# A graph layer on one core: 68 instead of 72 column copies on VectorE, a second bank for the turned comparison, and a later addition of the sums

## The chip, the core and the metric

The kernel runs on one core of a Trainium2 chip. The metric is the device time of one execution in microseconds (us); the median of the runs is given. The engines are TensorE (PE), VectorE (DVE), ScalarE (ACT), GpSimd (POOL) and SyncE (SP). Each takes its instructions in order from a queue of its own; what orders them among each other are semaphores.

## What is computed

12500 nodes have 64 features each (x), and 400000 edges, sorted by their destination, have 16 attributes each.

```python
m_in = concat([x[src], x[dst], edge_attr], axis=-1)     # 64 + 64 + 16
h = silu(m_in @ W1 + b1)
messages = silu(h @ W2 + b2)
agg = segment_sum(messages, dst, num_segments=12500)
z = silu(concat([x, agg], axis=-1) @ W3 + b3)
out = layernorm(x + z, axis=-1)
```

## The kernel before

The edges are cut into 3125 tiles of 128, and eight tiles make an **oct**: 391 turns of the main loop, whose order on PE, ACT, VectorE and SP is written out by hand (`tc.manual_schedule`). Two tiles make a **pair**, and pairs are laid side by side over the 128 partitions.

Since the edges are sorted, the eight tiles of an oct point at a short window of 48 nodes. `compare_nodes` (L433, VectorE) compares each edge's destination with the 48 and gives a 0/1 matrix `eh`; `turn` (L451, PE) turns it into a PSUM bank (`ph`, pool `psh`), and `turned` (L461, VectorE) copies that to SBUF. `window_product` (L410, PE) multiplies the window's slice of x with its part of W1 into a bank of the pool `mis`, and `window_copy` (L415, VectorE) takes it out. `first_layer` (L486, L489, L490 on PE; L493, the silu to `h`, on ACT) adds the three parts of the first layer; `second_layer` (L502, L504 on PE; L508, the silu to `m`, on ACT) follows two octs later. `add_up` (L517, PE) sums the messages of an oct into one of four slots of a PSUM bank (`sums`, pool `psa`), four octs later; `add_window` (L522, VectorE) adds such a slot to the window's place in `agg`, LAST octs later, with an address from a register.

The sources' features come in three ways, and this is what the engines are mostly busy with:

- POOL gathers 128 rows of x (from oct 12 on, of the product x·W1, made once by `table`, L186 on PE and L189 on ACT, and written to DRAM) with one indirect DMA (L386), one for each tile.
- For some first pairs of an oct, ACT and VectorE copy the columns from x in SBUF one by one, four bytes on 64 partitions: `nc.scalar.copy` (L312) and a `tensor_reduce` over one element (L310). Each address is loaded into a register first (L302): 16 registers at once on ACT, up to 32 on VectorE. `address` (L371, VectorE) makes addresses of 256 indices, one pair. Each pair done in this way saves POOL two gathers.
- For one second pair in sixteen octs, SP fetches the rows singly, 16 in each oct.

How many columns an oct copies is set by two tuples, and the place of VectorE's parts in the loop by their order:

```python
ACOLS = (40, 32)
VCOLS = (32, 0, 32, 8)
RATE = sum(ACOLS) + sum(VCOLS)          # columns per oct, 256 to a pair
...
columns(o, ENG.DVE, 0)                  # behind add_window, compare_nodes
first_layer(o)
window_copy(o + 1)
columns(o, ENG.DVE, 1)
turned(o + 1)
columns(o, ENG.DVE, 2)
columns(o, ENG.DVE, 3)
```

So VectorE's order in oct o is: `bases` (registers for the windows' places, every fourth oct, L395), `add_window`, `compare_nodes` of oct o + 2, 32 columns, `window_copy` of oct o + 1, `turned` of oct o + 1, 32 and 8 columns, then node work and `address`. PE's order is: `turn` and `window_product` of oct o + 1, `first_layer` of o, `add_up` of o - 4, `second_layer` of o - 2, then node work (L548, L553, L558), which is spread over the octs for groups of 512 nodes whose sums are complete.

The eight PSUM banks are: `mis` 2 (window products; in the first twelve octs also `table`'s products and the gathered features that are turned, `pt`), `wrow` 1, `ps1` 2, `ps2` 1, `psh` 1, `psa` 1.

The functions that the diff touches:

Of the kernel before, what the change touches and what calls it, by code (L numbers as in the profile page):

```python
# [9 lines left out]
F32 = mybir.dt.float32  # L10
# [6 lines left out]
PSUM = bass.MemoryType.PSUM  # L17
# [3 lines left out]
P = 128  # L21
G = 4
CT = 24
OT = 8
# [3 lines left out]
AHEAD = 3  # L28
SECOND = 2
THIRD = 4  # L30
LAST = 6
RAW = 12
BEGIN = 6
TABLES = 7
ACOLS = (40, 32)
VCOLS = (32, 0, 32, 8)
ROWS = 16
LOADS = (16, 32)
XADDR = 37344
# [64 lines left out]
def windows(ctx, tc, ident, identb, badi, pa, x, xt, xt2, src_c, src_row, dst_c, dst_row, attr_t, attr_2, base, w1, b1, w2, b2, w3, b3, out, edges):  # L104
# [5 lines left out]
    NO = base.shape[1]  # L110
# [63 lines left out]
    zero = const.tile([P, 1], F32, name="zero")  # L174
    nc.vector.memset(zero, 0.0)

    mis = ctx.enter_context(tc.tile_pool(name="mis", bufs=2, space=PSUM))


    def table(c):  # L180
# [79 lines left out]
    with tc.tile_pool(name="gat", bufs=AHEAD + 2) as gat, \  # L260
# [3 lines left out]
            tc.tile_pool(name="msg", bufs=THIRD - SECOND + 1) as msg, \  # L264
            tc.tile_pool(name="ps1", bufs=2, space=PSUM) as ps1, \
            tc.tile_pool(name="ps2", bufs=1, space=PSUM) as ps2, \
            tc.tile_pool(name="psh", bufs=1, space=PSUM) as psh, \
            tc.tile_pool(name="psa", bufs=1, space=PSUM) as psa, \
            tc.tile_pool(name="cx", bufs=5) as cx, tc.tile_pool(name="cxi", bufs=3) as cxi, \
            tc.tile_pool(name="rx", bufs=2) as rx, tc.tile_pool(name="rxi", bufs=2) as rxi, \  # L270
# [193 lines left out]
        def first_layer(o):  # L464
            c, t0, n, first, last = octs[o]
            n2 = n + n % 2
            k = n2 // 2
            ga = got.pop(o)
            oh, eh = hots.pop(o)
            p1 = ps1.tile([P, OT // 2, P], F32, name="p1")  # L470
            if o < RAW:
                c = 1 if o in pairs else 0
                nc.tensor.matmul(p1[:, :k], xw[o % 3], oh, start=True, stop=False, skip_group_check=True)
                if c:
                    nc.tensor.matmul(p1[:, 0, :], w1d, cols.pop(o), start=False, stop=False, skip_group_check=True)
                pt = mis.tile([P, OT // 2, P], F32, name="mm")
                for i in range(c, k):
                    nc.tensor.transpose(pt[:, i, :], ga[:, 2 * i:2 * i + 2, :].rearrange("p s d -> p (s d)"), ident)
                xg = msg.tile([P, OT // 2, P], F32, name="m")
                nc.vector.tensor_copy(xg[:, c:k], pt[:, c:k])  # L480
                nc.tensor.matmul(p1[:, c:k], w1d, xg[:, c:k], start=False, stop=True, skip_group_check=True)
            else:
                c = 1 if o in pairs else 0
                for i in range(c, k):
                    g2 = single.pop(o) if o in rpairs and i == 1 else ga[:, 2 * i:2 * i + 2, :]
                    nc.tensor.matmul(p1[:, i, :], g2.rearrange("p s d -> p (s d)"), ident,  # L486
                                     is_transpose=True, start=(i == c), stop=False, skip_group_check=True)
                if c:
                    nc.tensor.matmul(p1[:, 0, :], w1d, cols.pop(o), start=False, stop=False, skip_group_check=True)  # L489
                nc.tensor.matmul(p1[:, :k], xw[o % 3], oh, start=False, stop=True, skip_group_check=True)  # L490
            columns(o, ENG.Activation, 0)
            h = work.tile([P, OT // 2, P], F32, name="h")
            nc.scalar.activation(h[:, :k], p1[:, :k], AF.Silu)  # L493
            made[o] = h, eh
# [25 lines left out]
        def add_window(o):  # L520
            a = agg[:, ds(winreg.pop((ENG.DVE, o)), S)]
            nc.vector.tensor_tensor(a, a, sums[:, o % 4, :], op=OP.add)  # L522
# [85 lines left out]
        for q in range(rest):  # L608
            o = lead[due[q]] + LAST - 1
# [40 lines left out]
        def times(lags):  # L650

            at = {}
            for o in range(NO):
                at.setdefault(o + lags.get(NO - 1 - o, lags[None]), []).append(o)
            return at

        seconds = times({None: SECOND, 0: 1, 1: 1, 2: 1})
        adds = times({None: THIRD, 0: 2, 1: 2, 2: 2, 3: 3, 4: 3, 5: 3})
        folds = times({None: LAST, 0: 3, 1: 4, 2: 4, 3: 5})

        for o in range(min(AHEAD, NO)):
            gather(o)
# [14 lines left out]
        with tc.manual_schedule(engines={ENG.PE, ENG.Activation, ENG.DVE, ENG.SP}):  # L677
# [4 lines left out]
            for o in range(NO + 2):  # L682
                if o == 0:
                    sources(0, slice(CT, SCT))
                    nc.sync.dma_start(dc[:, CT:SCT], dst_c[:, CT:SCT])
                for k in parts[3 * o - 3:3 * o] if o else []:
                    n = min(XC, NP - k)
                    nc.scalar.activation(agg[:, k:k + n], zero.to_broadcast([P, n]), AF.Copy)
                if o < 2:
                    for c in parts[2:5] if o == 0 else parts[5:]:  # L690
                        resident(c)
                if o == 3:
                    for s in range(2):
                        nc.scalar.dma_start(w3s[s * D:(s + 1) * D, :], w3[D:2 * D, :])
                    nc.scalar.dma_start(w3x, w3[0:D, :])
                    nc.vector.tensor_copy(b3r, b2p[:, 1:2, :].to_broadcast([3, G, D]))
                if o == 8:
                    nc.scalar.dma_start(dc[:, SCT:], dst_c[:, SCT:])
                if o == RAW:
                    nc.vector.memset(mv, 1.0)  # L700
                    nc.vector.memset(eps, 1e-5)
                index(o + 3)
                rload(o + 3)
                if o % (SCT // OT) == 6 and (o // (SCT // OT) + 1) * SCT < TILES:
                    sources(o // (SCT // OT) + 1)
                if o + AHEAD < NO:
                    gather(o + AHEAD)
                if o + 3 < NO and octs[o + 3][3]:
                    load(octs[o + 3][0])
                if o + 3 < NO:  # L710
                    window_load(o + 3)
                if o + 1 < NO:
                    turn(o + 1)
                if o + 1 < NO - 1:
                    window_product(o + 1)
                if o % 4 == 0 and 4 <= o < NO + 4:
                    bases(ENG.DVE, o - 4)
                for q in folds.get(o, []):
                    add_window(q)
                if o == 1:  # L720
                    relative(CT, SCT)
                if o + 2 < NO:
                    compare_nodes(o + 2)
                columns(o, ENG.DVE, 0)
                if o < NO:
                    first_layer(o)
                for f, a in todo.get(o, []) if o < NO else []:
                    if f is node_silu:
                        f(*a)
                if o == 0:  # L730
                    nc.vector.tensor_copy(b2r, b2p[:, 0:1, :].to_broadcast([3, OT, D]))
                if o + 1 < NO:
                    if o + 1 < NO - 1:
                        window_copy(o + 1)
                    if o + 1 == NO - 2:
                        window_product(o + 2)
                        window_copy(o + 2)
                    columns(o, ENG.DVE, 1)
                    turned(o + 1)
                    columns(o, ENG.DVE, 2)  # L740
                columns(o, ENG.DVE, 3)
                if 10 <= o < 9 + len(cuts):
                    relative(cuts[o - 10], cuts[o - 9])
                if 30 <= o < 30 + 2 * LP and o % 2 == 0:
                    k = (o - 30) // 2
                    part = rel[:, k * TILES // LP:(k + 1) * TILES // LP]
                    nc.vector.tensor_reduce(lims[:, 0, k:k + 1], part, AX.X, OP.min)
                    nc.vector.tensor_reduce(lims[:, 1, k:k + 1], part, AX.X, OP.max)
                if o >= 1:
                    for c in tables[(o - 1) * per:o * per]:  # L750
                        table(c)
                for q in adds.get(o, []):
                    add_up(q)
                for q in seconds.get(o, []):
                    second_layer(q)
                for f, a in todo.get(o, []) if o < NO else []:
                    if f in (node_begin, node_x, node_sums):
                        f(*a)
                address(o + 2)
                raddress(o + 2)  # L760
                rows(o)
                if o < NO:
                    for f, a in todo.get(o, []):
                        if f not in (node_silu, node_begin, node_x, node_sums):
                            f(*a)
                if o == NO - 4:
                    for q in range(rest, NG):
                        node_load(q)
                if o in (NO - 3, NO - 2):
                    for q in (rest,) if o == NO - 3 else range(rest + 1, NG):  # L770
                        node_begin(q, acc if q == rest else mis.tile([P, G, D], F32, name="mm"))
                        for i in range(G):
                            node_x(q, i)
# [279 lines left out]
```

## Time and profile before

| | |
|---|---|
| median of 3 runs | 3539.86 us (3532.58 to 3542.2) |
| the profiled execution | 3546.66 us, of which the span in the profile is 3544.8 us |
| busy share PE / DVE / ACT / POOL | 73% / 72% / 89% / 71% |
| granted clock of PE, mean | 0.671 |
| octs | 391 |

In the profile's rows a group has its line, engine, operation, its tiles (out<-in), shapes and count, then the busy time in us and the mean duration of one in ns, and behind the second bar the engine's idle time ahead of these instructions and what ended it. "issue" is idle time that no wait in the profile accounts for. Rows of the order of time begin with the start and the duration in us; in brackets stands the idle time ahead of them. Rows of the stretches give the stretch, its length, then busy time and number of instructions for PE, weight loads, DVE, ACT and POOL, PE's granted clock, and the DMA share and rate. Rows of a line's instructions give the count, the shortest, median and longest duration in ns, and the first and last start in us. An engine's name with a q (DVEq) stands for its queue: register loads, register arithmetic and waits, which count as no busy time. Register loads are named by L302 (column addresses) and L395 (windows' places).

### The profile page before, as it was taken

The page shows a single profiled execution, that of the slowest core. Times are in us where ns is not written, and L with a number is a line of the kernel's source. Part 1 is how long each engine was busy: PE and PEld are TensorE (multiplying, and loading weights), DVE is VectorE, ACT ScalarE, POOL GpSimd, SP SyncE. Part 2 cuts the span into 40 slices and gives each one's busy share as a digit, 9 for nine tenths or more (in the row PEclk, how much of TensorE's full clock was granted, in tenths as well). Part 3 has the DMA queues.
Part 4 walks back from the last instruction along what each step waited for, and adds up shares of the span by engine and source line. Part 5 has one row for each costly group of instructions (what it writes and reads, how often), then busy time and mean ns, then how long its engine had stood idle before and what let it go on. Part 6 is the DMA issues. An engine that isn't in the chain of part 4 may idle for free. (4 is left out here: it accounts for less than half of the span.)

```text
span 3544.8 us, 111270 instructions
## 1 busy us (share of the span) xinstructions
PE 2574.5 (73%) x15317; PEld 1760.8 (50%) x15317; DVE 2549.4 (72%) x29217; ACT 3167.6 (89%) x27861; POOL 2512.8 (71%) x2666
## 2 busy tenths in 40 slices
PE   7777777877777677777766777777777767766676
PEld 5454454545444455454544544544545444544454
DVE  2777777777777777777777777777777777777772
ACT  2899999999999999999999999999999999999992
POOL 7777776777767767767677677776776777767774
PEclk7766766566667666666676666666666666677666
DMA  5222211212211212111211211112211111112121
GB/s 110 58 41 40 41 39 38 40 36 41 40 41 41 41 37 41 38 37 38 45 42 37 41 38 38 39 39 42 43 39 37 39 40 38 38 40 44 38 41 30
DMA packets 159534, 147.84 MB, mean 42 GB/s; under 512 B 103191, under 2 KB 111532, under 8 KB 158268
## 3 DMA queue, kind: packets, MB, share of 16 engines
q0 software_dynamic: 85024, 87.23, 14.0%
q1 hardware_dynamic: 59670, 45.36, 5.0%
q10 hardware_dynamic: 14086, 8.03, 1.0%
q14 instruction: 627, 5.14, 0.5%
q8 instruction: 127, 2.08, 0.2%
HBM read 133.98 MB, written 6.40 MB: 40 GB/s over the span
## 5 line engine op out<-in xcount | busy, mean ns | idle before, releaser
L386 POOL DMA_INDIRECT ga<-pa,sc x2563 | 2421.8, 945 | 959.5 <-issue 681.6
L312 ACT COPY cx<-xs 64x4 uint8 x27016 | 2709.9, 189 | 150.7 <-issue 122.3
L310 DVE TENSOR_REDUCE cx<-xs 64x4 uint8 x27000 | 1821.9, 140 | 830.9 <-issue 789.7
L451 PE MATMUL ph<-identb,eh 128*96 128x128 bf16 x1563 | 229.0, 291 | 627.0 <-DVE oh L461 618.4
L517 PEld LDWEIGHTS pg<-eh,m 128*64 128x64 f32 x6250 | 289.1, 179 | 769.8 <-DVE agg L522 714.2
L490 PE MATMUL p<-oh,xw 128*128 128x512 f32 (+1 forms) x758 | 651.8, 960 | 0.0
L504 PE MATMUL p<-w2d,h 128*128 128x128 f32 x3126 | 626.8, 362 | 0.0
L504 PEld LDWEIGHTS p<-w2d,h 128*128 128x128 f32 x3126 | 531.3, 257 | 128.4 <-issue 128.4
L517 PE MATMUL pg<-eh,m 128*64 128x48 f32 x6250 | 343.9, 266 | 237.1 <-DVE agg L522 230.1
L451 PEld LDWEIGHTS <-eh 128*96 128x96 bf16 x1563 | 158.4, 169 | 700.2 <-DVE oh L461 689.2
L493 ACT ACTIVATE h<-p 128x512 f32<-128x512 f32 x391 | 232.2, 594 | 110.0 <-PE p L490 88.6
L486 PE MATMUL p<-ident,ga 128*128 128x128 f32 x1282 | 319.9, 384 | 5.2 <-DMA ga<-pa,sc 5.2
L508 ACT ACTIVATE m<-p 128x512 f32<-128x512 f32 x391 | 231.6, 592 | 49.6 <-PE p L504 44.1
L461 DVE COPY oh<-ph 96x512 f32<-96x512 f32 x391 | 263.7, 674 | 5.2 <-PE ph L451 5.2
L486 PEld LDWEIGHTS p<-ident,ga 128*128 128x128 f32 x1282 | 245.1, 206 | 5.9 <-issue 5.8
L410 PE MATMUL mm<-w1bb,xr 65*96 65x128 f32 x782 | 237.3, 401 | 9.1 <-DMA xr<-in_xt 5.6
L433 DVE TENSOR_TENSOR eh<-wrow,dc 128x384 f32<-128x384 f32 x392 | 213.4, 545 | 4.8 <-PE pg L517 4.6
L502 PE MATMUL p<-b2r,one 3*128 3x512 bf16 x391 | 189.6, 485 | 1.7 <-ACT m L508 1.6
L490 PEld LDWEIGHTS p<-oh,xw 128*128 128x128 f32 x758 | 188.3, 304 | 0.0
L410 PEld LDWEIGHTS mm<-w1bb,xr 65*96 65x96 f32 x782 | 150.4, 246 | 10.8 <-DMA xr<-in_xt 6.0
L415 DVE TENSOR_TENSOR xw<-mm,mask 96x128 f32<-96x128 f32 x391 | 109.5, 280 | 22.7 <-PE mm L410 19.6
L489 PE MATMUL p<-cx,w1d 128*128 128x128 f32 x420 | 121.5, 388 | 0.0
(96 smaller groups left out, 921.7 us busy)
## 6 DMA issues: line engine op xcount, KB each, us to landing
rx<-pa SPq DMA_DIRECT2D x5888, 0.2 KB
ga<-pa,sc POOLq DMA_INDIRECT x2563
oh<-in_attr SPq DMA_DIRECT2D x130, 192.0 KB
xr<-in_xt SPq DMA_DIRECT2D x391, 24.0 KB
cxi<-in_src_row SPq DMA_DIRECT2D x211, 1.0 KB
xs<-in_xt ACTq DMA_DIRECT2D x6, 512.0 KB
pa<-v ACTq DMA_DIRECT2D x12, 256.0 KB
xa<-in_x SPq DMA_DIRECT2D x24, 128.0 KB
```

Of the source, the lines that this page charges most:

```text
L310: nc.vector.tensor_reduce(to, frm[:, :, None], AX.X, OP.max)
L312: nc.scalar.copy(to, frm)
L386: nc.gpsimd.indirect_dma_start(out=ga[:, i, :], out_offset=None, in_=x if o < RAW else pa[:, :], in_offset=bass.IndirectOffsetOnAxis(ap=sc ...
L410: nc.tensor.matmul(pw[:E, :], winrow[o], w1bb.rearrange("k s m -> k (s m)"), start=True, stop=True)
L451: nc.tensor.matmul(ph[:E, i, :], eh[:, i, :, 1], identb, start=(i == 0), stop=(i == k - 1), skip_group_check=True)
L461: nc.vector.tensor_copy(oh[:E, :], ph[:E, :(n + 1) // 2].rearrange("p i e -> p (i e)"))
L486: nc.tensor.matmul(p1[:, i, :], g2.rearrange("p s d -> p (s d)"), ident, is_transpose=True, start=(i == c), stop=False, skip_group_check=True)
L490: nc.tensor.matmul(p1[:, :k], xw[o % 3], oh, start=False, stop=True, skip_group_check=True)
L493: nc.scalar.activation(h[:, :k], p1[:, :k], AF.Silu)
L504: nc.tensor.matmul(p2[:, 2 * i:2 * i + 2, :].rearrange("p s d -> p (s d)"), h[:, i, :], w2d, start=False, stop=(i == k - 1), skip_group_ch ...
L508: nc.scalar.activation(m[:, :n2], p2[:, :n2], AF.Silu)
L517: nc.tensor.matmul(pg[s * D:(s + 1) * D, :], m[:, i, :], eh[:, i // 2, :, s], start=(i < 2), stop=(i >= n - 2), skip_group_check=True)
```

## The change

VectorE copies 68 columns in each oct where it copied 72: the last part of VCOLS has 4 columns for 8. With that RATE is 140, so a pair's 256 columns take 1.83 octs. `psh` has two banks and `mis` one; in the first twelve octs the gathered features are turned in a bank of `psh`. `add_window` moves in VectorE's order from ahead of `compare_nodes` to behind `turned`, and LAST, the number of octs after which it is due, falls from 6 to 5 (with its exceptions at the end, `folds`); the node work that needs the sums is placed by LAST and comes an oct earlier.

```diff
-LAST = 6
+LAST = 5
...
-VCOLS = (32, 0, 32, 8)
+VCOLS = (32, 0, 32, 4)
...
-    mis = ctx.enter_context(tc.tile_pool(name="mis", bufs=2, space=PSUM))
+    mis = ctx.enter_context(tc.tile_pool(name="mis", bufs=1, space=PSUM))
...
-            tc.tile_pool(name="psh", bufs=1, space=PSUM) as psh, \
+            tc.tile_pool(name="psh", bufs=2, space=PSUM) as psh, \
...
-                pt = mis.tile([P, OT // 2, P], F32, name="mm")
+                pt = psh.tile([P, OT // 2, P], F32, name="ph")
...
-        folds = times({None: LAST, 0: 3, 1: 4, 2: 4, 3: 5})
+        folds = times({None: LAST, 0: 3, 1: 3, 2: 4})
...
                 if o % 4 == 0 and 4 <= o < NO + 4:
                     bases(ENG.DVE, o - 4)
-                for q in folds.get(o, []):
-                    add_window(q)
                 if o == 1:
                     relative(CT, SCT)
...
                     columns(o, ENG.DVE, 1)
                     turned(o + 1)
+                for q in folds.get(o, []):
+                    add_window(q)
+                if o + 1 < NO:
                     columns(o, ENG.DVE, 2)
                 columns(o, ENG.DVE, 3)
```

## The prediction

> **What bounds the kernel now.** I read the busy shares first, then the two middle stretches of the span, the groups of that stretch, who waits for whom there, and last one oct (eight tiles of 128 edges, one turn of the main loop) in order of time.
>
> ```profile
> PE 2574.5 (73%) x15317; PEld 1760.8 (50%) x15317; DVE 2549.4 (72%) x29217; ACT 3167.6 (89%) x27861; POOL 2512.8 (71%) x2666
> 1000.00:2000.00 1000.00, 727.20 (x4315) 496.77 (x4316) 741.91 (x8637) 928.74 (x8266) 711.69 (x754) 0.66 0.20 40
> 2000.00:3000.00 1000.00, 723.84 (x4315) 493.89 (x4315) 740.13 (x8632) 927.35 (x8263) 711.03 (x753) 0.67 0.20 39
> ```
>
> ACT looks like the bound with 89%, and the two stretches are alike, so one oct from the middle speaks for all. The groups between 1000 and 3000 us tell more:
>
> ```profile
> L310 DVE TENSOR_REDUCE cx<-xs 64x4 uint8 x16056 | 1083.5, 140 | 498.0 <-issue 477.2 <-ACT h L493 13.7 <-ACT cx L312 1.4
> L461 DVE COPY oh<-ph 96x512 f32<-96x512 f32 x223 | 150.4, 675 | 0.0
> L312 ACT COPY cx<-xs 64x4 uint8 x16060 | 1610.9, 189 | 90.0 <-issue 73.7 <-DVE oh L461 5.9 <-DVE xw L415 1.6
> L493 ACT ACTIVATE h<-p 128x512 f32<-128x512 f32 x224 | 133.1, 594 | 43.1 <-PE p L490 39.2
> L508 ACT ACTIVATE m<-p 128x512 f32<-128x512 f32 x223 | 132.1, 593 | 10.7 <-PE p L504 7.4 <-ACT cx L312 0.2
> ...
> L386 POOL DMA_INDIRECT ga<-pa,sc x1507 | 1424.0, 945 | 577.6 <-issue 398.9 <-PE p L486 140.2 <-DMA ga<-pa,sc 32.7
> ```
>
> L461 runs once an oct: 2000 / 223 = 8.97 us per oct. VectorE is busy for (741.91 + 740.13) / 223 = 6.65 us of it and idle for "issue" for 477.2 / 223 = 2.14 us: 8.79 of 8.97 us, with next to no wait for another engine. What "issue" is shows in one oct of VectorE, and in the register loads of its queue (the 64x4-byte column copies take their addresses from registers, L302), which count as no busy time:
>
> ```profile
> 1509.76 0.21 DVE L522 TENSOR_TENSOR agg<-agg,pg 128x48 f32 x1 [0.26 <-DVE cx L310]
> 1509.88 0.55 DVE L433 TENSOR_TENSOR eh<-wrow,dc 128x384 f32<-128x384 f32 x1
> 1512.02 2.12 DVE L310 TENSOR_REDUCE cx<-xs 64x4 uint8 x32 [1.60 <-issue]
> 1514.07 0.27 DVE L415 TENSOR_TENSOR xw<-mm,mask 96x128 f32<-96x128 f32 x1
> 1514.27 0.67 DVE L461 COPY oh<-ph 96x512 f32<-96x512 f32 x1
> 1515.73 2.67 DVE L310 TENSOR_REDUCE cx<-xs 64x4 uint8 x40 [0.79 <-issue]
> 1518.32 0.27 DVE L371 TENSOR_SCALAR cxi<-cxi 1x256 int32<-1x256 int32 x1
> 1518.52 0.19 DVE L522 TENSOR_TENSOR agg<-agg,pg 128x48 f32 x1
> ```
>
> ```profile
> L302 DVEq TENSOR_LOAD <-cxi x1: 2104/2104/2104, 1509.8 to 1509.8; - x1
> L302 DVEq TENSOR_LOAD <-cxi x1: 2100/2100/2100, 1513.5 to 1513.5; - x1
> L302 DVEq TENSOR_LOAD <-cxi x1: 596/596/596, 1517.1 to 1517.1; - x1
> L302 DVEq TENSOR_LOAD <-cxi x1: 2097/2097/2097, 1518.4 to 1518.4; - x1
> L395 DVEq TENSOR_LOAD <-bi x56: 341/344/352, 1007.6 to 2980.7; - x56
> ```
>
> The loads of 32, 32 and 8 registers take 2.10, 2.10 and 0.60 us, 4.8 us per oct. Between the end of the first (1511.9) and the start of the second (1513.5) the queue passes 34 instructions (32 reduces, L415, L461) in 1.6 us, 47 ns each; after the second (1515.6 to 1517.1) 32 in 1.5 us, again 47 ns. From load to load around, 1509.8 to 1518.4, there is no hole: VectorE's queue is full. It is the bound, hidden behind a share of 72%.
>
> **The change part by part.**
>
> *Four columns fewer.* The load of 8 registers becomes one of 4; L395 above loads 4 in 0.344 us, so 0.60 - 0.34 = 0.25 us. Four reduces less to pass: 4 x 0.047 = 0.19 us. Together 0.44 us per oct. At 140 columns per oct (144 so far) and 256 per pair of tiles, 205 pairs (211) are filled in 205 x 256 / 140 = 375 octs: 0.44 x 375 = 165 us. If only the engine's own time counted, it would be 4 x 2.12 / 32 = 0.27 us, 99 us; if VectorE weren't the bound, nothing. I take 165, since the queue has no hole.
>
> *Six pairs fewer.* Each pair spares POOL two gathers, so there are 3125 - 2 x 205 - 2 x 23 = 2669 of them (2657 so far).
>
> ```profile
> 2.82 1.11 POOL L386 DMA_INDIRECT ga<-in_x,sc  x1 [1.33 <-DMA sc<-in_src_c]
> ...
> 3500.39 0.94 POOL L386 DMA_INDIRECT ga<-pa,sc  x1 [0.30 <-issue]
> 3501.63 0.94 POOL L386 DMA_INDIRECT ga<-pa,sc  x1 [0.30 <-issue]
> ```
>
> One costs 0.945 + 0.30 = 1.245 us, with the steps of the timeline up to 1.25. Twelve more are 15 us, hidden while POOL waits (140.2 us for PE in the 2000 above). It sets a floor, however: 2.8 us, 2669 gathers, and the 43.2 us that now follow the last start (3544.8 - 3501.63) give a span of 3369 to 3382 us. Per oct: 8 - 2 x 140/256 - 2 x 16/256 = 6.78 gathers (16 rows an oct come by SP), 8.44 to 8.48 us.
>
> *add_window behind the turned copy, one oct earlier.* VectorE's queue passes the same entries, only behind L461 instead of ahead of L433: the load that now starts at 1513.5 comes later and the one at 1518.4 earlier, by the same time. Queued behind it are 36 reduces, and PE's add_up waits for it. I cost it at 0; its price otherwise is a rival below. LAST = 5 moves the node sums one oct forward with it: 0.
>
> *Two banks for the turned comparison.*
>
> ```profile
> PE ph L451 <- DVE oh L461: 376.1, 205, 3.2
> PE pg L517 <- DVE agg L522: 135.8, 145, 2.8
> ```
>
> PE waits twice an oct, 1.7 us for the copy that frees the one bank and 0.6 us for add_window. The first wait goes; the second stays and moves behind the copy, where it becomes longer. Since PE isn't the bound, this is worth 0 by itself, but it is what makes the late add_window bearable. The chain to be late next is add_window, add_up, second layer, turn, window product, L415, L461, add_window. At PE's slow pace:
>
> ```profile
> 1518.83 1.10 PE L517 MATMUL pg<-eh,m 128*64 128x48 f32 x16
> 1519.86 0.60 PE L502 MATMUL p<-b2r,one 3*128 3x512 bf16 x1
> 1520.40 2.08 PE L504 MATMUL p<-w2d,h 128*128 128x128 f32 x8
> 1523.69 0.66 PE L451 MATMUL ph<-identb,eh 128*96 128x128 bf16 x4 [1.22 <-DVE oh L461]
> 1524.14 0.69 PE L410 MATMUL mm<-w1bb,xr 65*96 65x128 f32 x2
> 1524.62 1.06 PE L486 MATMUL p<-ident,ga 128*128 128x128 f32 x4
> 1525.48 1.90 PE L490 MATMUL p<-oh,xw 128*128 128x512 f32 x2
> ...
> 1540.06 0.73 PE L553 MATMUL wrow<-w3x,xs 64*128 64x64 f32 x2
> ```
>
> 1.03 + 0.54 + 2.08 + 0.73 (node work, in some octs) + 0.45 + 0.69, then 0.20 + 0.67 + 0.20 on VectorE: 6.6 us against a period of 8.53. PE alone, from 1518.83 to 1527.38 without its wait of 1.22: 7.33, with node work 8.06. Both fit.
>
> *One bank for products of slices of x.* In steady state L415 reads it before PE comes round: 0. In the first octs the node table uses it too:
>
> ```profile
> 44.24 5.66 PE L186 MATMUL mm<-w1ab,xs 64*128 64x64 f32 x32
> 46.53 0.59 ACT L189 COPY v<-mm 128x512 f32<-128x512 f32 x1 [0.66 <-PE mm L186]
> ```
>
> The second table of an oct must now wait for the first one's copy, about 0.7 us, six times: +4 us (0 if other work covers it, 10 if the window product is held too).
>
> *What is next.* POOL at 8.44 to 8.48 us, and ACT: (928.74 + 927.35) / 223 = 8.32 us busy, 8.65 if its 73.7 / 223 = 0.33 us of "issue" stays. When ACT doesn't wait it does without:
>
> ```profile
> 1531.81 0.60 ACT L508 ACTIVATE m<-p 128x512 f32<-128x512 f32 x1
> 1540.23 0.60 ACT L508 ACTIVATE m<-p 128x512 f32<-128x512 f32 x1
> SPq L366 <- ACTq L302: 261.0, 98, 7.3
> ```
>
> 8.42 us from second silu to second silu. SP has 261 / 223 = 1.2 us to spare. With three engines within 0.1 us of VectorE's 8.53 I allow 0.05 us per oct for their getting in each other's way (bounds 0 and 0.12, which is ACT's 8.65): +19 us.
>
> Sum against the profiled execution, 3546.7 us (span 3544.8): 3546.7 - 165 + 4 + 19 = 3405. That execution lies 7 us above the median of the runs, so 3398 us.
>
> **The rivals.**
>
> *ACT takes over at 8.65 us.* For it: 0.33 us of "issue" today. Against: the 8.42 above. 0.32 x 375 = 120 us less, 3546.7 - 120 + 4 - 7 = 3424. Chance 0.21.
>
> *PE becomes the bound.* If a denser PE were granted less clock, 8.06 us plus a few late gathers could reach 8.75: 0.22 x 375 = 82, 3461. The clock of 0.66 has room downward. Chance 0.10.
>
> *VectorE falls out of the way altogether* and POOL's floor decides: span 3369 to 3382, 3364 to 3377 as a median. Chance 0.07.
>
> *ACT is the bound already.* Then VectorE's columns are off the path, ACT copies 72 as before, and the time stays at 3540. Against: ACT idles 144 us of 2000, 50 of them for PE, and VectorE's queue has no hole. Chance 0.05. [...]
>
> *The moved add_window holds VectorE's queue.* Its register arithmetic and its wait now stand right ahead of a 2.10 us load. If the queue stopped there until the copy had ended (1514.94) instead of loading from 1513.5, each oct would lose 1.4 us and win 0.44: +0.96 x 375 = 360, 3900 us. It is slower from a hold of 0.44 us on. Against: today the load starts at 1518.4, before L371 has ended and before L522 starts, so the queue runs past both. Chance 0.09, with smaller holds.
>
> **How the numbers follow.** Forecast 0.48; with the first three rivals 0.86 faster, 0.05 same (within 0.3%, about what a measurement can tell), 0.09 slower. The range runs from POOL's floor, 3368, past the PE rival's 3461, to 3470.
>
> **What would show it.** The load that precedes the last reduces near 0.34 us; L461 to L461 at 8.5 to 8.6 us; PE's wait for L461 gone and the one for L522 near 2 us; POOL's wait for L486 small; VectorE's "issue" little below 2 us. It is wrong if L415 or L461 waits for PE, if the load behind L522 starts only when L461 has ended, or if ACT shows no wait for PE and a period over 8.6.

## The result, and the profile after

The changed kernel takes 3525.34 us (median of 20 runs), the one before 3541.43 (20): a ratio of 0.9956, interval 0.9943 to 0.9969. It is faster, as forecast, but by 16 us and not by 140. Some of the runs below were made on chips on which the kernel before takes 5296 to 5412 us; these are given as ratios to the kernel before on the same chip and are called runs with the stall (for the pauses shown in the last section).

The page's busy shares of the changed kernel, its two middle stretches, and its groups between 1000 and 3000 us:

```profile
PE 2568.4 (73%) x15311; PEld 1882.0 (53%) x15311; DVE 2435.7 (69%) x27691; ACT 3160.7 (89%) x27845; POOL 2526.8 (72%) x2678
```

```profile
1000.00:2000.00 1000.00, 725.66 (x4337) 537.30 (x4336) 714.12 (x8243) 933.57 (x8323) 719.61 (x762) 0.69 0.20 40
2000.00:3000.00 1000.00, 723.66 (x4325) 529.44 (x4326) 710.36 (x8214) 929.45 (x8294) 717.69 (x761) 0.69 0.20 40
```

```profile
L310 DVE TENSOR_REDUCE cx<-xs 64x4 uint8 x15241 | 1022.2, 140 | 512.5 <-issue 495.8 <-ACT m L508 8.3 <-ACT h L493 3.0
L461 DVE COPY oh<-ph 96x512 f32<-96x512 f32 x224 | 151.1, 675 | 0.0
L433 DVE TENSOR_TENSOR eh<-wrow,dc 128x384 f32<-128x384 f32 x225 | 123.3, 548 | 55.7 <-PE wrow L553 37.5 <-PE wrow L558 12.8 <-issue 1.4
...
L508 ACT ACTIVATE m<-p 128x512 f32<-128x512 f32 x225 | 133.6, 594 | 56.1 <-PE p L504 52.9
L493 ACT ACTIVATE h<-p 128x512 f32<-128x512 f32 x224 | 132.4, 591 | 2.7
```

L461 runs once an oct. It still comes only 224 times in 2000 us, 8.93 us apart (8.97 before). VectorE's reduces are fewer, but its "issue" has grown from 477 to 496 us where it should have shrunk. L433, `compare_nodes`, which waited 0.2 us in the kernel before, now waits 55.7. Its row in the kernel before:

```profile
L433 DVE TENSOR_TENSOR eh<-wrow,dc 128x384 f32<-128x384 f32 x224 | 122.3, 546 | 0.2 <-issue 0.2
```

Who waits for whom in the changed kernel, in the same stretch:

```profile
PE pg L517 <- DVE agg L522: 550.2, 224, 6.2
...
POOL ga L386 <- PE p L486: 123.3, 83, 3.3
...
ACT m L508 <- PE p L504: 52.9, 81, 1.4
DVE eh L433 <- PE wrow L553: 37.5, 43, 1.3
DVE eh L433 <- PE wrow L558: 12.8, 26, 1.0
```

PE's two waits have become one, 550.2 / 224 = 2.46 us in every oct, for add_window. What L433 waits for is PE's node work (L553, L558) on the tile `wrow`, 37.5 + 12.8 = 50.3 of its 55.7 us. The row of 48 numbers that L433 reads and the accumulator that the node work writes are different columns of that tile, which is one PSUM bank.

One oct of this kind in order of time, VectorE first, then PE, then the register loads of VectorE's queue:

```profile
1526.74 0.19 DVE L522 TENSOR_TENSOR agg<-agg,pg 128x48 f32 x1
1527.16 2.58 DVE L310 TENSOR_REDUCE cx<-xs 64x4 uint8 x36 [0.23 <-issue]
1529.98 0.28 DVE L371 TENSOR_SCALAR cxi<-cxi 1x256 int32<-1x256 int32 x1 [0.24 <-issue]
1531.09 0.56 DVE L433 TENSOR_TENSOR eh<-wrow,dc 128x384 f32<-128x384 f32 x1 [0.83 <-PE wrow L553]
1533.29 2.12 DVE L310 TENSOR_REDUCE cx<-xs 64x4 uint8 x32 [1.64 <-issue]
```

```profile
1526.99 0.87 PE L517 MATMUL pg<-eh,m 128*64 128x48 f32 x16 [3.41 <-DVE agg L522]
1527.79 0.60 PE L502 MATMUL p<-b2r,one 3*128 3x512 bf16 x1
1528.32 2.08 PE L504 MATMUL p<-w2d,h 128*128 128x128 f32 x8
1530.33 0.73 PE L553 MATMUL wrow<-w3x,xs 64*128 64x64 f32 x2
```

```profile
L302 DVEq TENSOR_LOAD <-cxi x1: 347/347/347, 1529.0 to 1529.0; - x1
L302 DVEq TENSOR_LOAD <-cxi x1: 2098/2098/2098, 1531.1 to 1531.1; - x1
```

PE starts add_up (L517) only once add_window is done, so its second layer and node work now end 4.1 us behind add_window (1526.93 to 1531.06). VectorE comes to L433 0.83 us earlier and is held; and the 2.10 us load behind it begins at 1531.1, with L433 and not ahead of it. In an oct where nothing holds L433 the load comes first, at 1513.4 for an L433 at 1514.15:

```profile
1514.15 0.53 DVE L433 TENSOR_TENSOR eh<-wrow,dc 128x384 f32<-128x384 f32 x1
```

```profile
L302 DVEq TENSOR_LOAD <-cxi x1: 2097/2097/2097, 1513.4 to 1513.4; - x1
```

So such an oct pays twice, for the wait and for a load that starts later and so runs beside less of VectorE's work. Worked out from the trace between 600 and 3300 us: L433 waits over 0.15 us in 108 octs, 0.65 us on average, and the load then starts 14 ns behind it (median; within 41 ns in 101 of them). In the other 195 octs the load starts 0.18 us ahead of L433 (median).

### The profile page after: what moved, and what is told of

It is laid out like the page before. It is cut to its first block, busy times and chain, and to the rows that moved or that the text cites. A ratio compares the mean times of both kernels' runs of the same rounds, so it can differ in the third digit from the quotient of the medians.

```text
span 3533.0 us, 109531 instructions
## 1 busy us (share of the span) xinstructions
PE 2568.4 (73%) x15311; PEld 1882.0 (53%) x15311; DVE 2435.7 (69%) x27691; ACT 3160.7 (89%) x27845; POOL 2526.8 (72%) x2678
## 3 DMA queue, kind: packets, MB, share of 16 engines
q8 instruction: 127, 2.08, 0.2%
## 5 line engine op out<-in xcount | busy, mean ns | idle before, releaser
L310 DVE TENSOR_REDUCE cx<-xs 64x4 uint8 x25480 | 1708.6, 140 | 852.1 <-issue 820.7
L517 PEld LDWEIGHTS pg<-eh,m 128*64 128x64 f32 x6250 | 284.9, 177 | 1362.2 <-DVE agg L522 1351.4
L517 PE MATMUL pg<-eh,m 128*64 128x48 f32 x6250 | 340.9, 265 | 907.2 <-DVE agg L522 905.8
L504 PE MATMUL p<-w2d,h 128*128 128x128 f32 x3126 | 727.9, 406 | 0.0
L504 PEld LDWEIGHTS p<-w2d,h 128*128 128x128 f32 x3126 | 619.2, 294 | 137.7 <-issue 137.7
L490 PE MATMUL p<-oh,xw 128*128 128x512 f32 (+1 forms) x758 | 565.5, 840 | 0.0
L486 PE MATMUL p<-ident,ga 128*128 128x128 f32 x1288 | 330.8, 396 | 7.2 <-DMA ga<-pa,sc 7.2
L433 DVE TENSOR_TENSOR eh<-wrow,dc 128x384 f32<-128x384 f32 x392 | 215.1, 549 | 113.5 <-PE wrow L553 61.1
L461 DVE COPY oh<-ph 96x512 f32<-96x512 f32 x391 | 263.7, 675 | 6.5 <-PE ph L451 6.5
L486 PEld LDWEIGHTS p<-ident,ga 128*128 128x128 f32 x1288 | 263.3, 218 | 8.4 <-issue 5.3
L410 PE MATMUL mm<-w1bb,xr 65*96 65x128 f32 x782 | 254.9, 427 | 9.1 <-DMA xr<-in_xt 9.0
L451 PEld LDWEIGHTS <-eh 128*96 128x96 bf16 x1563 | 201.4, 188 | 16.6 <-DVE eh L433 3.0
L490 PEld LDWEIGHTS p<-oh,xw 128*128 128x128 f32 x758 | 182.8, 296 | 0.0
L410 PEld LDWEIGHTS mm<-w1bb,xr 65*96 65x96 f32 x782 | 163.6, 266 | 11.1 <-issue 5.6
L415 DVE TENSOR_TENSOR xw<-mm,mask 96x128 f32<-96x128 f32 x391 | 110.0, 281 | 26.3 <-PE mm L410 23.2
```

The source lines that it names most:

```text
L310: nc.vector.tensor_reduce(to, frm[:, :, None], AX.X, OP.max)
L410: nc.tensor.matmul(pw[:E, :], winrow[o], w1bb.rearrange("k s m -> k (s m)"), start=True, stop=True)
L451: nc.tensor.matmul(ph[:E, i, :], eh[:, i, :, 1], identb, start=(i == 0), stop=(i == k - 1), skip_group_check=True)
L461: nc.vector.tensor_copy(oh[:E, :], ph[:E, :(n + 1) // 2].rearrange("p i e -> p (i e)"))
L504: nc.tensor.matmul(p2[:, 2 * i:2 * i + 2, :].rearrange("p s d -> p (s d)"), h[:, i, :], w2d, start=False, stop=(i == k - 1), skip_group_ch ...
L517: nc.tensor.matmul(pg[s * D:(s + 1) * D, :], m[:, i, :], eh[:, i // 2, :, s], start=(i < 2), stop=(i >= n - 2), skip_group_check=True)
```

## The experiments

**Theory:** the late add_window moves PE's node work to where compare_nodes, which reads from the same bank, must wait for it, and VectorE's queue with its register load stands still behind compare_nodes. **Rivals:** PE's one meeting with VectorE makes the second silu late (ACT's 52.9 us); the four columns are worth little anyway; the late add_window or the banks cost by themselves.

The table gives the mean distance from one add_window to the next between 600 and 3300 us, worked out from each trace, for octs in which PE does node work and for the others; all on chips without the stall. It is to be read down each column: also where nothing is held, the two kinds of oct differ in length.

| kernel | octs with node work | others | median, us | ratio to before (interval) |
|---|---|---|---|---|
| before | 8.84 | 9.09 | 3541.43 | 1 |
| changed | 9.08 | 8.74 | 3525.34 | 0.9956 (0.9943 to 0.9969) |
| changed, again | 9.11 | 8.74 | 3528.35 | 0.9967 (0.9954 to 0.9980) |
| changed, banks exchanged | 8.32 | 8.73 | 3384.55 | 0.9558 (0.9539 to 0.9576) |
| before, 68 columns alone | 8.33 | 8.78 | 3390.12 | 0.9583 (0.9559 to 0.9608) |
| changed, compare_nodes later | 8.36 | 8.79 | 3403.39 | 0.9613 (0.9586 to 0.9640) |
| changed, 72 columns | 9.26 | 9.08 | 3631.60 | 1.0264 (1.0237 to 1.0290) |
| the same, banks exchanged | 8.81 | 9.04 | 3537.08 | 0.9993 (0.9980 to 1.0006) |

**Banks exchanged.** The changed kernel, but the node accumulator no longer lies beside the row; the sums' slots do:

```diff
-        sums = psa.tile([P, 4, S], F32, name="pg")
+        sums = wrow[:, 256:256 + 4 * S].rearrange("p (q s) -> p q s", q=4)
-        acc = wrow[:, 256:256 + G * D].rearrange("p (i d) -> p i d", i=G)
+        acc = psa.tile([P, G, D], F32, name="pg")
```

> The changed kernel, with the sums' four slots in the bank of wrow (beside the row of 48 numbers that compare_nodes reads) and the node accumulator in the bank that the sums had. Theory of the held comparison: after the change compare_nodes stands about 3.7 us behind add_window and must wait for PE's node matmuls into the bank that its row lies in; while it waits, VectorE's queue doesn't begin the 2.1 us register load behind it. Some 0.7 us in each of about 190 octs with node work make 130 us. Without the shared bank that goes: 3525 - 130 = about 3395 us (3380 to 3415), octs with node work at 8.4 us instead of 9.08, and no wait of L433 for L553 or L558. Rival, PE's single meeting with VectorE makes the second silu late (ACT waited 53 us for L504 in 2000, where it was 7): the bank plays no part, 3515 to 3530 us, and ACT's wait stays near 50. Rival, the four columns are worth far less than 165 us anyway: also about 3525.

That run fell on a chip with the stall: 5203 us, 0.9828 (0.9803 to 0.9854). Put again:

> The changed kernel with the sums' slots and the node accumulator exchanged between their banks, as before; in the first run all engines' queues stalled between single instructions and even the kernel before took 5296 us, so the question is put again. Theory of the held comparison: 3380 to 3415 us, octs with node work at about 8.4 us, no wait of L433 for L553 or L558. Rivals (second silu late; columns worth little): 3515 to 3530 us.

Measured 3384.55 us, as the theory had it. Octs with node work fall from 9.08 to 8.32 us, and the others stay where they were (8.74 and 8.73). The groups between 1000 and 3000 us, and two of the waits:

```profile
L386 POOL DMA_INDIRECT ga<-pa,sc x1592 | 1504.5, 945 | 496.0 <-issue 418.8 <-DMA ga<-pa,sc 54.2 <-PE p L486 15.0
...
L310 DVE TENSOR_REDUCE cx<-xs 64x4 uint8 x15944 | 1068.9, 140 | 505.6 <-issue 439.1 <-ACT m L508 37.8 <-ACT cx L312 20.2
...
L461 DVE COPY oh<-ph 96x512 f32<-96x512 f32 x235 | 158.4, 674 | 0.0
...
L433 DVE TENSOR_TENSOR eh<-wrow,dc 128x384 f32<-128x384 f32 x234 | 127.3, 544 | 5.5 <-PE p L504 1.6 <-PE p L486 1.0 <-issue 0.7
```

```profile
PE wrow L517 <- DVE agg L522: 542.0, 221, 6.2
...
ACT m L508 <- PE p L504: 15.6, 25, 1.4
```

L433 waits 5.5 us and for no node work; "issue" is 439.1 / 235 = 1.87 us an oct. PE's one meeting with VectorE is nearly as long as in the changed kernel (542 us against 550), so that rival is out; ACT's wait for L504 shrank from 52.9 to 15.6 us without anything done about it, so it came with the hold. POOL waits 15 us for PE (L486) and is near the floor of the prediction.

**68 columns alone**, in the kernel before:

```diff
-VCOLS = (32, 0, 32, 8)
+VCOLS = (32, 0, 32, 4)
```

> The kernel before with 68 columns on VectorE alone; banks, place of add_window and LAST as before. Theory of the held comparison: in the old order compare_nodes comes right behind add_window, some 5 us after PE's node work, so nothing is held and the full 0.44 us per oct come out: 3541 - 165 + up to 20 = 3376 to 3400 us. Rival, the four columns are worth little because ACT, POOL or PE is next within a tenth of a us: 3480 to 3530 us.

With the stall 5246 us, 0.9899 (0.9877 to 0.9922). Again:

> The kernel before with 68 columns alone, put again for the same reason. Theory of the held comparison: 0.44 us in each of 375 octs, 3376 to 3400 us. Rival, the four columns are worth little because ACT, POOL or PE is next: 3480 to 3530 us.

Measured 3390.12 us, 149 less than the kernel before on the same chip. The four columns are worth what the sum gave them, and the banks and the late add_window aren't needed for it. In its waits the old order still shows PE standing twice in an oct, at no cost that the time shows (0.9583 against 0.9558 with one wait, the intervals overlap):

```profile
PE ph L451 <- DVE oh L461: 421.4, 222, 3.2
...
PE pg L517 <- DVE agg L522: 100.2, 102, 2.8
```

**68 columns and the banks**, add_window in its old place (the edit above and the three lines on `mis`, `psh` and `pt` of the change).

> The kernel before with 68 columns and with the two banks for the turned comparison and one for products of slices of x, add_window in its old place and LAST = 6. Theory of the held comparison: as the columns alone, and up to 6 us more for the node table at the start, which now has one bank: 3380 to 3406 us; PE's wait for L461 gone, its wait for L522 longer. Rival, PE's waits count: 10 to 30 us less than the columns alone. Rival, the columns are worth little: about 3520.

> The kernel before with 68 columns and the banks of the change, add_window in its old place. The columns alone gave 3390 us, with POOL hardly ever waiting. Theory of the held comparison: the banks cost nothing but the start, 3385 to 3405 us. Rival, the single bank for products of slices of x holds window_product in every oct: 3420 or more.

Both runs met the stall: 0.9941 (0.9920 to 0.9962) and, on another chip, 0.9913 (0.9897 to 0.9930). On the first chip the columns alone took 15 us less (5246 against 5261; the intervals just touch), where a price of up to 6 for the banks was expected. Nothing speaks for a gain by the banks; what they cost this kernel without the stall stays open.

**72 columns, banks and late add_window**: the changed kernel with VCOLS as before.

> The changed kernel with 72 columns on VectorE as before (8 in the last part): banks and late add_window alone. Theory of the held comparison: with 8 columns in the last part compare_nodes comes 0.44 us later behind add_window, about 4.1 us, so it still waits in the octs in which PE's node work ends at 4.35 us: 10 to 60 us slower than before, with 6 of it at the start, 3550 to 3600. Rival, the order costs as much as with 68 columns: 3541 + 145 = about 3685. Rival, the order costs nothing: 3541 to 3547.

> Banks and late add_window alone, 72 columns. Theory of the held comparison: compare_nodes comes 0.44 us later behind add_window than with 68, so it is held more rarely: 3550 to 3610 us. Rival, the order costs what it costs with 68 columns (3525 - 3385 = 140): about 3680. Rival, it costs nothing: 3541 to 3547.

> Banks and late add_window alone, 72 columns; put again where the queues don't stall. Theory of the held comparison: held more rarely than with 68, 3550 to 3610 us. Rival, the order costs the same 140 us: about 3680. Rival, nothing: 3541 to 3547.

With the stall 1.0183 (1.0152 to 1.0213), 1.0141 (1.0124 to 1.0158) and 1.0156 (1.0139 to 1.0173). Without it:

> Banks and late add_window alone, 72 columns. Theory of the held comparison, without stalls: 3550 to 3610 us. Rival, the order costs the same 140 us: about 3680.

Measured 3631.60 us: slower, above the 3550 to 3610 that I had given the theory and below the rival's 3680. That size was wrong. The hold is indeed rarer (82 octs between 600 and 3300 us, where the changed kernel has 108), but it costs more than I had allowed:

```profile
L433 DVE TENSOR_TENSOR eh<-wrow,dc 128x384 f32<-128x384 f32 x218 | 119.1, 546 | 28.4 <-PE wrow L553 16.4 <-PE wrow L558 6.7 <-PE ph L451 1.6
```

28.4 us of waiting in 218 octs are 0.13 us each, while the kernel lost 90 / 391 = 0.23 us an oct. I put the rest down to the load that starts late; no run measures that share by itself.

**The same with banks exchanged** (both edits above).

> As the kernel with banks and late add_window alone, 72 columns, but with the sums' slots and the node accumulator exchanged between their banks. Theory of the held comparison: nothing is held, so the order costs only the start: 3541 to 3555 us. Rival, the late add_window costs by itself: as without the exchange.

With the stall 0.9979 (0.9964 to 0.9993). Without:

> The same with sums' slots and node accumulator exchanged between their banks. Theory of the held comparison, without stalls: 3541 to 3555 us. Rival, the late add_window costs by itself: as without the exchange.

Measured 3537.08 us, not to be told from the kernel before. So with the banks exchanged the late add_window, LAST = 5 and the second bank together cost nothing and bring nothing in the whole; the hold is 3631.60 - 3537.08 = 95 us here.

**compare_nodes later**, behind VectorE's first 32 columns, the banks left as in the change:

```diff
+                columns(o, ENG.DVE, 0)
                 if o + 2 < NO:
                     compare_nodes(o + 2)
-                columns(o, ENG.DVE, 0)
```

> The changed kernel with its banks as they are, but compare_nodes behind VectorE's first 32 columns instead of ahead of them, some 7.5 us behind add_window. Theory of the held comparison: PE's node work, over 4.4 us behind add_window, is done by then and nothing is held: 3380 to 3410 us. Rival, the bank by itself is at fault and not the place: about 3525.

With the stall 0.9836 (0.9819 to 0.9852), and once more:

> The changed kernel with compare_nodes behind VectorE's first 32 columns, banks as in the change; put again where the queues don't stall. Theory of the held comparison: 3380 to 3410 us. Rival, the bank by itself is at fault and not the place: about 3525.

0.9853 (0.9833 to 0.9873). Without it:

> The changed kernel with compare_nodes behind VectorE's first 32 columns, banks as in the change. Theory of the held comparison, without stalls: 3380 to 3410 us (with stalls, as before, 0.985 of the kernel before). Rival, the bank by itself is at fault: like the changed kernel beside it.

Measured 3403.39 us, 125 less than the changed kernel on the same chip:

> The changed kernel itself, beside the others on the same chip. Without stalls 3525 us, 0.9956 of the kernel before; with stalls, by the theory of the held comparison, clearly above the kernels in which nothing is held (0.983 to 0.985 there), near 0.995 to 1.00.

That one took 3528.35 us. Where compare_nodes stands some 7 us behind add_window, it is not held in any oct though the bank is shared (2.0 us of idle time ahead of L433 between 1000 and 3000 us, none of it put down to PE): bank and place together make the hold. The kernel is still 19 us slower than the one with the banks exchanged (0.9613 against 0.9558, the intervals don't overlap); what these 19 us are stays open.

## Why the prediction failed

*What bounds the kernel:* right. VectorE's queue of register loads and passed instructions was the bound at a busy share of 72%; taking 0.44 us per oct of it away gave 149 us in the kernel before, where the sum had 165 less 19 for crowding. The engine's own time alone, by the prediction's sum, would have given 99.

*Four columns fewer:* right in size. The load of 4 registers takes 0.347 us in the trace after.

*Six pairs, POOL's floor:* right. The span is 3384.5 us with the banks exchanged and 3376.8 with the columns alone; the floor was put at 3369 to 3382.

*One bank for products of slices of x, and the start:* the wait came as forecast, 0.7 us for the first table's copy:

```profile
64.65 2.11 PE L186 MATMUL mm<-w1ab,xs 64*128 64x64 f32 x16 [0.68 <-ACT v L189]
```

Its sum of +4 us was small for the start. The turned copy of oct 12 begins at 147.1 to 151.0 us in the six traces of kernels with the banks and without the stall, and at 142.9 (before) and 137.4 (68 columns alone) without the banks: 4 to 14 us, of the banks and the late add_window together. In the whole they came out at 0 (3537 against 3541 us).

*add_window behind the turned copy, cost 0:* this step failed. I followed its entries on VectorE's queue and the chain that returns to L415, 6.6 us against 8.53, but not every reader of what PE writes on the way. compare_nodes now starts 3.7 us behind add_window (median) instead of right behind it; PE's add_up follows add_window in every oct, and with it went the second layer and the node work. By the numbers of the prediction the node work ends 1.03 + 0.54 + 2.08 + 0.73 = 4.4 us behind add_window at PE's slow pace; compare_nodes, whose row lies in the accumulator's bank, is ready as early as 3.1 us behind it (the earliest twentieth in the changed kernel's trace). In the old order it came nearly a whole oct behind the add_window that let that node work start, which is why no row of the trace before showed that dependence. The prediction named three signs of being wrong; none of them looked at compare_nodes, and in the middle of the trace none came. The price is 144 us (3528.35 - 3384.55, on two chips on which the kernel before takes 3541 and 3539), nearly all of the 149 won. That the changed kernel came out faster at all, as forecast, is therefore luck: a gain that I had and a price that I hadn't nearly cancel.

*The rival of the held queue* was close in kind and wrong in place: not add_window's own wait holds the load, but that of compare_nodes behind it. What I held against it, that the queue runs past L371 and L522, was seen on instructions that waited for no other engine, and says nothing of one that does. Its point of decision, a hold of 0.44 us per oct, fits: the changed kernel loses 0.42 (8.93 less 2000 / 235 = 8.51) and stays 0.04 under the kernel before.

*The rival that ACT is the bound already:* ACT is busy for 89% of the span in both kernels and for 93% with the banks exchanged and with the columns alone; it wasn't the bound of the kernel before, as the columns alone show: ACT copies as many columns per oct as before, and the time fell. The prediction's 50 us of ACT waiting for PE are 39.2 + 7.4 = 46.6 by its rows; nothing hangs on it.

*The rival of a slower clock:* that a denser PE is granted less clock was a supposition, and no run shows it. PE's mean granted clock was 0.671 before, 0.691 in the changed kernel, 0.697 with the columns alone and 0.718 with the banks exchanged.

## What to carry to other kernels

When an instruction is moved, list everything that then follows it on the other engines, and for each bank that these write, every reader, also one that reads other columns of it. Here L433 waited 50.3 us between 1000 and 3000 us for writes to other columns of its bank; in the same stretch of the trace before it waited 0.2 us, none of it for PE, and no row there shows that dependence. Change one thing at a time where parts don't need each other; here the first of three edits alone was worth nine times all three. An engine's busy share can hide that it is the bound: VectorE was busy for 72%, and its queue loaded registers for 4.8 us in each oct of 8.97.

## What the runs showed of the hardware

Where L433 waited over 0.15 us, the register load behind it did not begin before it: the load began 14 ns after L433's start (median of 108 octs of the changed kernel), although in the oct shown above the trace shows nothing else on the queue for 1.5 us ahead of it. In the other 195 octs the load began 0.18 us ahead of it (median).

This kernel's waits did not go by the columns: in the changed kernel L433 waits 50.3 us between 1000 and 3000 us for node work that writes other columns of its tile, which is one bank, and not at all for that work when it writes another tile in another bank (banks exchanged). No run tells the tile from the bank, and none shows what would happen without these waits.

PE's pace moved with the place of its waits. The second layer's matmuls (L504) took 363 ns each between 1000 and 3000 us of the trace before and 408 after, while L490, later behind the wait, went from 966 to 840 ns. Within the changed kernel's trace L504 took 386 ns on average in octs in which PE had waited 1 to 2 us for add_window, and 430 where it had waited longer. add_up itself (L517), which comes first behind the wait, took 266 and 264. Why, no run here shows.

On three of the five chips of these experiments the kernel before took half as long again (5296, 5403 and 5412 us, where it took 3539 and 3541 on the other two). In the kernel with 68 columns alone on one of the three, VectorE idles ahead of its column copies for "issue" for 1153.8 us between 1500 and 4500 us, and ACT for 876.4 us (477.2 and 73.7 us in 2000 us of the trace before); POOL's "issue" did not grow (388.6 us in these 3000, 398.9 in the 2000). In stretches VectorE pauses between single copies:

```profile
2002.87 0.21 DVE L310 TENSOR_REDUCE cx<-xs 64x4 uint8 x2 [1.25 <-issue]
2003.60 0.15 DVE L310 TENSOR_REDUCE cx<-xs 64x4 uint8 x1 [0.52 <-issue]
2004.31 0.15 DVE L310 TENSOR_REDUCE cx<-xs 64x4 uint8 x1 [0.56 <-issue]
```

These are reduces that in the traces before and after follow each other every 0.064 us (median of the steps within a row of them). No run here shows why they pause. On each of these chips the kernels came in the same order as without the stall, with smaller differences: from 0.983 to 1.018 of the kernel before, where they have 0.956 to 1.026 without it.
